# One Trainium2 core, a scan block and a window-attention block: first image's phase reordered, PSUM banks taken from the plan, three planned lengths changed

## The chip, the cores and the metric

The kernel runs on one core of one Trainium2 chip. The metric is the device time of one execution in microseconds. Engines are named as in the profile: PE (matmul; PEld is its weight load), DVE (vector), ACT (scalar), POOL (GpSimd) and SP, which issues most DMAs.

## The reference

Eight images of 192 channels, 64 x 64, float32, go through two layers.

Layer 0 widens 192 to 384 channels with a 1x1 product, convolves each channel 3x3, and derives from the result a 16-channel proxy. Four gates per direction and channel come from the proxy by 1x1 products. A recurrent scan then runs in four directions over chunks of eight columns:

```
x = conv1x1(x, W_in)
x = depthwise_conv3x3(x, W_dw) + b_dw
x_proxy = conv1x1(x, W_xd)
Gl, Gm, Gr = normalize_w(...)                  # each divided by |Gl|+|Gm|+|Gr|+eps
hn = l * x + gl * h_up + gm * h + gr * h_dn    # eight steps, four directions
out = out * Us + xs * Ds
y = einsum('bdchw,d->bchw', out_y, w_m); layernorm over channels; grn; conv1x1 to 192
```

Layer 1 is a layer norm, attention in 8 x 8 windows with six heads of 32 (the 16 largest scores of each row are kept, the others set to -100), a projection, a second layer norm, and a feed-forward part of 768 with gelu.

## The kernel before

**The first image's phase.** Image 0 is projected and convolved in a phase of its own, written out by hand. There are three blocks of 128 channels (`ct`) and four units of 16 rows (`u`), so twelve units. `projected` (L430 to L443) is four products into a PSUM tile `pin` (two buffers) and an ACT copy into the padded image `full`. `convolved` (L462 to L471) makes nine DVE steps of 1024 elements per partition into `acc` (three buffers). `convolved_by_products` (L473 to L484) makes the convolution with 18 products instead, each with a diagonal weight `dg`, into two PSUM tiles `pc`, emptied by ACT. `stored` (L446 to L457) copies `acc` twice with ACT, in two orders, and SP writes them to DRAM as `xsT` and `xs`. Nine units go to DVE, and the last three (`ct` 2, `u` 1 to 3) to PE. The loop at the end alternates: one projection, then the convolutions that have their rows; the three product units come last. The nine `dg` steps (L487) stand ahead of the loop on ACT's queue. Weights are loaded by `load`, which takes SP's and ACT's queue in turn.

**The weight work (L504 to L576).** In pools of its own, behind the phase: `w_cv` from `w_dw`, factors put into `w_g2` and `w_out`, and bias rows made by small products on PE (`bias_row`) and written back into the weight tiles by SP.

**The planned part.** Everything after that is written as steps with an engine, a planned length, what they read and what they write. `Plan.order` simulates the engines with these lengths, 60 times with adapted ranks, keeps the shortest plan and emits the steps sorted by planned start. Each engine then runs its instructions in that order. `front(b)` projects and convolves image b by way of DRAM (L650, L653, L696), `scan(b)` makes eight steps of twelve tiles (gates and outputs by L809, gate arithmetic L858 to L942, sums L968 to L990, `norm` L1003 to L1068), and `windows(b)` handles 8 rows of windows. The scan of image b stands beside the windows of image b-1 and the front of image b+1, so the first scan has no windows beside it and the last windows have no scan.

**PSUM.** Six banks (`l_ps`) serve all tiles of `bank()` under the tag "lp", two more (`n_ps`) the gate tile `nb`. The plan gives each new tile the bank that comes free first in its own times, but the program only asks the pool for the next buffer of that tag. The planned lengths are in nanoseconds:

```
vec = lambda n: (n / 0.96 + 69, 88)
act = lambda n, more=50.0: (n / 1.2 + more, 110)
gp = lambda n: (n * 2.3 + 52, 42)
```

`gp(512)` is the planned length of L897, L914, L918, L929, L980, L982, L988, L1406, L1423 and L1438; `mask` (L1393, L1396) is planned with 1500.

Of the kernel before, what the change touches and what calls it, by code (L numbers as in the profile page):

```python
# [31 lines left out]
P = 128  # L32
# [22 lines left out]
class Held:  # L55


    def __init__(self, pool, shape, name, bufs=None, tag=None, dtype=F32):
        self.args = pool, shape, dtype, name, tag or name, bufs or pool.bufs
        self.tag, self.bufs = (id(pool), tag or name), bufs or pool.bufs  # L60
        self.users, self.left, self.end, self.next, self.tile = [], 0, 0.0, None, None

    def make(self):
        if self.tile is not None:
            return
        pool, shape, dtype, name, tag, bufs = self.args
        self.tile = pool.tile(shape, dtype, name=name, tag=tag, bufs=bufs)

    def __call__(self):
# [10 lines left out]
class Plan:  # L80
# [67 lines left out]
    def order(self):  # L148

        before = [s.before for s in self.steps]
        tiles = {h: h.left for s in self.steps for h in s.held}
        best = None
        for n in range(self.RUNS):
            for s, k in zip(self.steps, before):
                s.before, s.ready = k, 0.0  # L160
            for h, k in tiles.items():
                h.left, h.end, h.next = k, 0.0, None
            run = self.run()
            if best is None or self.length < best[0]:
                best = self.length, run, [s.start for s in run]
            for s in run:
                needs = [d.start for d in s.after] + [h.next.start for h in s.held if h.next]
                rank = min(needs, default=s.end) - (s.end - s.start)
                s.rank = (s.rank + rank) / 2 if n else rank
        self.length, run, starts = best  # L170
        for s, t in zip(run, starts):
            s.start = t
        return run

    def run(self):
# [20 lines left out]
        for s in self.steps:  # L196
            for h in s.makes:
                queues.setdefault((h.tag, s.lane), []).append(s)
                slots.setdefault(h.tag, [(0.0, k, None) for k in range(h.bufs)])
        first = {k: 0 for k in queues}  # L200

        def kept(tag):
# [58 lines left out]
        while todo:  # L261
            for e in dirty_plain:
                best_plain[e] = picked(e, None, plain[e], ready)
            for e in dirty | dirty_plain:
                best[e] = picked(e, best_plain[e], makers[e], room)
            dirty_plain, dirty = set(), set()
            e = min((x for x in engines if best[x]), key=lambda x: best[x][1])
            _, t, s = best[e]
            s.start = t
            if e == "PE":  # L270
                lead, cycles, share = s.cost
                end = stream(t + lead, cycles, share)
                free[e], s.end = end, end + 140.0
            else:
                hold, more = s.cost
                free[e] = t + hold
                s.end = free[e] + more
            (makers if s.makes else plain)[e].remove(s)
            dirty_plain.add(e)
            todo -= 1  # L280
            done.append(s)
            for tag in needs.get(s, ()):
                first[tag, s.lane] += needs[s][tag]
            for h in s.makes:
                slot = min(slots[h.tag], key=lambda x: x[:2])
                slots[h.tag].remove(slot)
                if slot[2]:
                    slot[2].next = s
            touched = bool(s.makes)
            for h in s.held:  # L290
                h.left -= 1
                h.end = max(h.end, s.end)
                if not h.left:
                    slots[h.tag].append((h.end + self.HOP, h.users[0].n + h.bufs, h))
                    touched = True
            for d in s.after:
                d.before -= 1
                d.ready = max(d.ready, s.end + (self.HOP if d.engine != e else 30.0))
                if not d.before:
                    wake(d)  # L300
                    if not d.makes:
                        dirty_plain.add(d.engine)
                    elif d.lane:
                        dirty.add(d.engine)
                    else:
                        touched = True
            if touched:
                dirty.update(engines)
# [10 lines left out]
def tile_ss2d_then_window_attention(ctx: ExitStack, tc: tile.TileContext, a: dict, out: bass.AP):  # L319
# [8 lines left out]

    const = ctx.enter_context(tc.tile_pool(name="const", bufs=1))

    queues = [nc.sync, nc.scalar]
    n_loads = 0

    def load(name, src=None, rows=None):

        nonlocal n_loads
        src = a[name] if src is None else src
        shape = list(src.shape)
        t = const.tile([rows or shape[0]] + shape[1:], F32, tag=name, name=name)
        if rows:  # L340
            nc.gpsimd.memset(t[HALF:rows], 0.0)
        queues[n_loads % 2].dma_start(t[0 : shape[0]], src)
        n_loads += 1
        return t

    def blank(name, shape, value=None, engine=nc.gpsimd):
# [12 lines left out]
    ident = blank("ident", [P, P])  # L359
    make_identity(nc, ident)  # L360

    w_in = load("w_in")
    w_dv = load("w_dv")
    xa = epool.tile([P, H, W], F32, name="xa")
    xb = epool.tile([P, NG // 2, 8, W], F32, name="xb")
    for u in range(NG // 2):
        nc.sync.dma_start(xa[:, 16 * u : 16 * u + 16, :], x[0, 0:P, 16 * u : 16 * u + 16, :])
        for k in range(2):
            row = 16 * u + 8 * k
            nc.scalar.dma_start(xb[64 * k : 64 * k + 64, u], x[0, P:DM, row : row + 8, :])  # L370
        if u == 0:
            vecs = load("vecs")
    full = [epool.tile([P, H + 2, W + 2], F32, name=f"full{ct}") for ct in range(CT)]
    for t in full:
        nc.vector.memset(t[:, 0 : H + 2 : H + 1, :], 0.0)
# [50 lines left out]
        h.make()  # L426
    with early, tc.tile_pool(name="early_ps", bufs=2, space=PSUM) as early_ps:

        taps = [(dy, dx) for dy in range(3) for dx in range(3)]
        dg = epool.tile([P, 9, P], F32, name="dg")  # L430

# [30 lines left out]
        def convolved(ct, u):  # L462

            acc = epool.tile([P, 16, W], F32, name="acc", bufs=3)
            for n, tap in enumerate(taps):
# [2 lines left out]
                    nc.vector.tensor_scalar(acc, near(ct, u, *tap), w, b_dw[:, ct : ct + 1], ALU.mult, ALU.add)  # L468
                else:
                    nc.vector.scalar_tensor_tensor(acc, near(ct, u, *tap), w, acc, ALU.mult, ALU.add)  # L470
            stored(ct, u, acc)  # L471

        def convolved_by_products(ct, u):  # L473

            acc = epool.tile([P, 16, W], F32, name="acc", bufs=3)
            for k in range(2):
                pc = early_ps.tile([P, CH, W], F32, name="pc")
                for n, (dy, dx) in enumerate(taps):
# [4 lines left out]
                nc.scalar.activation(acc[:, 8 * k : 8 * k + 8, :], pc, AF.Identity, bias=b_dw[:, ct : ct + 1])  # L483
            stored(ct, u, acc)  # L484

        for n in range(9):
            nc.scalar.activation(dg[:, n, :], ident, AF.Copy, scale=w_dv[:, CT - 1, n : n + 1])  # L487
        units = [(ct, u) for ct in range(CT) for u in range(NG // 2)]
        by_vector = [(ct, u) for ct, u in units if ct < CT - 1 or u == 0]
        by_tensor = [c for c in units if c not in by_vector]  # L490
        done = 0
        for ct, u in units:
            projected(ct, u)
            while done < len(by_vector) and by_vector[done] < (ct, u):
                convolved(*by_vector[done])
                done += 1
            while by_tensor and by_tensor[0] < (ct, u):
                convolved_by_products(*by_tensor.pop(0))
        for c in by_tensor:
            convolved_by_products(*c)  # L500
        assert done == len(by_vector)

    with tc.tile_pool(name="prep", bufs=2) as prep, tc.tile_pool(name="prep_ps", bufs=2, space=PSUM) as prep_ps:

        w_dw = prep.tile([3 * RG, CT * 4 * 3], F32, name="w_dw")
        nc.sync.dma_start(w_dw, a["w_dw"])
        id3 = prep.tile([3 * RG, RG], F32, name="id3")
        nc.vector.tensor_add(id3, ident[0 : 3 * RG, 0:RG], ident[0 : 3 * RG, RG : 2 * RG])
        nc.vector.tensor_add(id3, id3, ident[0 : 3 * RG, 2 * RG : 3 * RG])
# [17 lines left out]
        def bias_row(name, dst, products, *more):  # L527

            n = dst.shape[-1]
            row = prep.tile([1, n], F32, name="row_" + name)  # L530
            nc.sync.dma_start(row, a[name])
            for at in range(0, n, 384):
                m = min(384, n - at)
                ps = prep_ps.tile([P, 512], F32, name="ps_pre")
# [3 lines left out]
                    )  # L538
                nc.vector.tensor_add(row[:, at : at + m], row[:, at : at + m], ps[0:1, 0:m])
            for extra in more:  # L540
                got = prep.tile([1, n], F32, name="more_" + name)
                nc.sync.dma_start(got, a[extra])
                nc.vector.tensor_add(row, row, got)
            nc.sync.dma_start(dst[HALF : HALF + 1, 1, :], row)


        bias_row("b_qk", w_qk, [(n1_b[:, ci : ci + 1], w_qk[0:HALF, ci, :]) for ci in range(2)])
# [39 lines left out]
    plan = Plan()  # L587
    vec = lambda n: (n / 0.96 + 69, 88)
    act = lambda n, more=50.0: (n / 1.2 + more, 110)
    gp = lambda n: (n * 2.3 + 52, 42)  # L590
    mm = lambda slots, n, share=0.96: (65.0, slots * n * 4.16, share)
    tiled = lambda cycles, share=1.0: (150.0, cycles, share)
    split = (275.0, 6475.0, 0.95)
# [550 lines left out]
    def window_row(b, g, z, sc, bb):  # L1144
# [225 lines left out]
        for r in range(3):  # L1370
# [21 lines left out]
            def mask(rng=rng, less=less):  # L1392
# [4 lines left out]
                    at()[:, rng, :], less(), neg.unsqueeze(1).to_broadcast([P, WS, 64])  # L1397
                )

            plan("DVE", (1500.0, 80.0), mask, r=kths, w=[less, (at, r)])  # L1400

            part = lambda rng=rng: at()[:, rng, :]
            plan(
# [15 lines left out]
            each = lambda v: v.unsqueeze(2).to_broadcast([P, WS, 64])  # L1419
            plan(  # L1420
                "POOL",
                gp(512),
                lambda part=part, rng=rng, each=each: nc.gpsimd.tensor_add(part(), part(), each(down()[:, rng])),  # L1423
                r=[(down, r)],
                w=[(at, r)],
# [3 lines left out]
            def denominators(part=part, rng=rng):  # L1429
# [4 lines left out]

            plan(
                "POOL",
                gp(512),
                lambda part=part, rng=rng, each=each: nc.gpsimd.tensor_mul(part(), part(), each(rd()[:, rng])),  # L1438
                r=[(rd, r)],
                w=[(at, r)],  # L1440
# [332 lines left out]
```

## Time and profile before

| what | value |
|---|---|
| median of 3 runs | 7621.01 us (7610.15 to 7637.82) |
| the profiled execution | 7623.82 us; its span 7622.0 us |
| mean granted PE clock | 0.86 |
| busy, share of the span | PE 88%, DVE 83%, POOL 82%, ACT 64% |
| first scan product (L809) to the last | 221.99 to 7066.16 us |
| DRAM traffic | 433.98 MB read, 226.18 MB written |

A line of the profile gives the source line, the engine, the operation, the tile written and the tiles read (buffer numbers left out). In answers in order of time the first two columns are start and duration, and the brackets hold the idle time ahead and what ended it. SPq and ACTq are DMA issues of those queues. Durations of single instructions overlap the next by some tens of ns, so a chain is read from start to start.

### The profile page before, as it was taken

The numbers are of one execution on the slowest core, as the hardware profiler recorded it, in microseconds if no ns is written. First come the engines' busy times: TensorE is split into PE (matmuls) and PEld (weight loads), VectorE is DVE, ScalarE is ACT, GpSimd is POOL, SyncE is SP. The second block draws the span as 40 slices with busy tenths as digits, with TensorE's granted clock in tenths as the row PEclk, the third lists the DMA queues.
The fourth block names the chain that finished last, engine by engine and source line by source line (L and its number), as shares of the span: only waits on it lengthen the run. The fifth ranks groups of instructions, "written<-read, shape, count | busy, mean of one in ns | idle before, by whom it ended". The sixth has DMA issues, their size and how long they took to land. (4 is left out here: it accounts for less than half of the span.)

```text
span 7622.0 us, 141764 instructions
## 1 busy us (share of the span) xinstructions
PE 6699.8 (88%) x50180; PEld 3458.4 (45%) x50180; DVE 6364.3 (83%) x15477; ACT 4896.1 (64%) x9649; POOL 6229.7 (82%) x6333
## 2 busy tenths in 40 slices
PE   5888789988998899888999899988888888888987
PEld 2333344444444444444444444444444444444554
DVE  5687788998899988988888988889899989889643
ACT  2455456765776657675777757766576756666665
POOL 0688888998899988988888888889899989899422
PEclk7888789987988889898998889988888878888999
DMA  3666455312551245312551135411211111111100
GB/s 107 164 174 163 121 139 135 101 51 75 154 145 46 55 134 151 89 46 78 157 139 47 50 105 143 124 50 46 60 50 50 49 59 52 49 45 45 32 22 14
DMA packets 988331, 669.39 MB, mean 88 GB/s; under 512 B 651972, under 2 KB 814215, under 8 KB 987623
## 3 DMA queue, kind: packets, MB, share of 16 engines
q1 hardware_dynamic: 985638, 656.86, 32.1%
q8 instruction: 398, 6.52, 0.4%
q10 hardware_dynamic: 1984, 3.48, 0.2%
q14 instruction: 311, 2.54, 0.1%
HBM read 433.98 MB, written 226.18 MB: 87 GB/s over the span
## 5 line engine op out<-in xcount | busy, mean ns | idle before, releaser
L809 PE MATMUL g<-xe,w_g 32*128 32x512 f32 x3648 | 1171.5, 749 | 224.4 <-DVE dx L968 74.6
L809 PE MATMUL g<-xo,w_g 32*128 32x512 f32 x3648 | 1189.1, 729 | 184.5 <-DVE dx L968 90.9
L866 ACT ACTIVATE ab<-g 128x512 f32<-128x512 f32 x1344 | 784.6, 596 | 393.0 <-PE nb L809 168.9
L897 POOL TENSOR_TENSOR ab<-ab 128x512 f32<-128x512 f32 x672 | 865.0, 1287 | 162.7 <-ACT ab L866 151.0
L929 POOL TENSOR_TENSOR pw<-pw,rr 128x512 f32<-128x512 f32 x672 | 867.4, 1291 | 135.6 <-ACT rr L912 115.4
L914 POOL TENSOR_TENSOR pw<-pw,pq 128x512 f32<-128x512 f32 x672 | 881.0, 1311 | 82.5 <-DVE pq L873 53.2
L918 POOL TENSOR_TENSOR pw<-pw,pq 128x512 f32<-128x512 f32 x672 | 878.1, 1307 | 15.5
L982 POOL TENSOR_TENSOR dx<-dx,hu 128x512 f32<-128x512 f32 x576 | 742.9, 1298 | 112.1 <-DVE hu L973 97.1
L910 ACT ACTIVATE rr<-nb,eps 128x512 f32<-128x512 f32 x672 | 462.0, 687 | 571.7 <-DVE nb L907 569.1
L809 PEld LDWEIGHTS g<-xo,w_g 32*128 32x128 f32 x3648 | 410.5, 208 | 719.3 <-DVE dx L968 192.9
L809 PEld LDWEIGHTS g<-xe,w_g 32*128 32x128 f32 x3648 | 408.9, 212 | 704.8 <-DVE dx L968 173.1
L1628 PE MATMUL lp<-hd,w_f 128*64 128x256 f32 (+1 forms) x2304 | 594.9, 497 | 56.1 <-ACT hd L1614 15.0
L990 POOL TENSOR_TENSOR y<-y,dx 128x512 f32<-128x512 f32 x384 | 597.6, 1563 | 2.2
L696 PE MATMUL lp<-strip,w_cv 128*32 128x256 f32 x8064 | 563.5, 418 | 27.6 <-DMA strip<-pad 19.2
L925 DVE SCALAR_TENSOR_TENSOR nb<-nb,rr 128x512 f32<-128x512 f32 x672 | 464.8, 692 | 142.5 <-ACT rr L912 140.3
L934 DVE SCALAR_TENSOR_TENSOR nb<-nb,pw 128x512 f32<-128x512 f32 x672 | 464.7, 692 | 138.4 <-POOL pw L929 136.2
L907 DVE TENSOR_TENSOR nb<-nb,ab 128x512 f32<-128x512 f32 x672 | 465.3, 692 | 113.1 <-POOL ab L897 103.5
L973 DVE TENSOR_TENSOR hu<-g,hid 128x512 f32<-128x512 f32 x768 | 518.7, 681 | 1.0 <-PE g L809 0.7
L809 PE MATMUL nb<-xe,w_g 32*128 32x512 f32 x672 | 479.1, 800 | 12.5 <-DVE hid L942 12.3
L888 ACT ACTIVATE nb<-nb 128x512 f32<-128x512 f32 x672 | 399.5, 594 | 137.7 <-DVE pq L875 78.2
L980 POOL TENSOR_TENSOR y<-hu,dx 128x512 f32<-128x512 f32 x192 | 246.3, 1289 | 291.7 <-DVE hu L973 289.7
L809 PE MATMUL nb<-xo,w_g 32*128 32x512 f32 x672 | 463.1, 774 | 14.6 <-DVE hid L942 14.6
(221 smaller groups left out, 16684.8 us busy)
## 6 DMA issues: line engine op xcount, KB each, us to landing
strip<-pad SPq DMA_DIRECT2D x1008, 132.0 KB
xd<-xsT SPq DMA_DIRECT2D x384, 256.0 KB
x<-xs SPq DMA_DIRECT2D x64, 768.0 KB
xd<-xs SPq DMA_DIRECT2D x192, 256.0 KB
z<-y SPq DMA_DIRECT2D x64, 768.0 KB
zg<-z SPq DMA_DIRECT2D x64, 768.0 KB
pad<-xin SPq DMA_DIRECT2D x168, 264.0 KB
xsT<-sn SPq DMA_DIRECT2D x168, 256.0 KB
```

Of the source, the lines that this page charges most:

```text
L696: nc.tensor.matmul(pc()[q * RG : (q + 1) * RG, k * 256 : (k + 1) * 256].rearrange("p (h w) -> p h w", h=4), lhsT=w_cv[:, ct, q, dx, :], rh ...
L809: nc.tensor.matmul(dst, lhsT=w[rows, col : col + P], rhs=xp[rows, :], start=True, stop=True)
L866: lambda r=r: nc.scalar.activation(ab()[:, r, :], g[r](), AF.Abs),
L897: plan("POOL", gp(512), lambda: nc.gpsimd.tensor_add(ab()[:, 0, :], ab()[:, 0, :], ab()[:, 1, :]), w=[ab])
L907: plan("DVE", vec(512), lambda: nc.vector.tensor_add(nb(), nb(), ab()[:, 0, :]), r=[ab], w=[nb])
L914: plan("POOL", gp(512), lambda: nc.gpsimd.tensor_add(one(), one(), pq()[:, 0, :]), r=[(pq, 0)], w=[pw])
L918: lambda: nc.gpsimd.tensor_add(one(), one(), pq()[:, 1, :]),
L929: plan("POOL", gp(512), lambda: nc.gpsimd.tensor_mul(one(), one(), rr()), r=[rr], w=[pw])
L973: lambda: nc.vector.tensor_mul(like(hu(), d), like(pu(), d), state(d, ct)),
L982: plan("POOL", gp(512), lambda: nc.gpsimd.tensor_add(dx(), dx(), hu()), r=[hu], w=[dx])
L990: nc.gpsimd.tensor_add(y, y, dx().rearrange("p (c i) -> p i c", c=CH))
L1628: nc.tensor.matmul(dst[:, at : at + rhs.shape[-1]], lhsT=lhsT, rhs=rhs, **flags)
```

## The change

Three edits, made together. Some helper lines move by a few; from the planned steps on (L600) the line numbers are the same in both.

1. *The first image's phase.* `load` uses SP's queue for all but `w_in`, `w_dv` and `vecs`, which go with the `xb` loads on ACT's. All twelve projections come first, with the `dg` steps behind the fourth. Then come the nine DVE convolutions, each followed by its store, and the three product units are put behind the 5th, 7th and 8th of them, with an own tag for their `acc`. The weight work keeps no pools of its own: it uses the phase's PSUM pool, and `w_dw` and the bias vectors are loaded early. The bias rows go back to the weight tiles from ACT's queue.
2. *The banks.* The plan notes which of the six banks it gave each tile (`slot`), and the program takes a tag with one buffer for each bank ("lp0" to "lp5").
3. *The lengths.* `gp` has 2.34 ns per element; the two POOL steps with a broadcast vector (L1423, L1438) get `gp_each` with 1.86; the mask is planned with 1700.

```diff
         pool, shape, dtype, name, tag, bufs = self.args
+        if tag == "lp":
+            tag, bufs = f"{tag}{self.slot}", 1
         self.tile = pool.tile(shape, dtype, name=name, tag=tag, bufs=bufs)
...
-                best = self.length, run, [s.start for s in run]
+                best = self.length, run, [s.start for s in run], {h: h.slot for h in tiles}
...
                 slot = min(slots[h.tag], key=lambda x: x[:2])
                 slots[h.tag].remove(slot)
+                h.slot = slot[3]
...
-        queues[n_loads % 2].dma_start(t[0 : shape[0]], src)
-        n_loads += 1
+        queue.dma_start(t[0 : shape[0]], src)
...
-    w_in = load("w_in")
-    w_dv = load("w_dv")
+    w_in = load("w_in", queue=nc.scalar)
+    w_dv = load("w_dv", queue=nc.scalar)
...
-        for n in range(9):
-            nc.scalar.activation(dg[:, n, :], ident, AF.Copy, scale=w_dv[:, CT - 1, n : n + 1])
...
-        for ct, u in units:
+        for n, (ct, u) in enumerate(units):
             projected(ct, u)
-            while done < len(by_vector) and by_vector[done] < (ct, u):
-                convolved(*by_vector[done])
-                done += 1
-            while by_tensor and by_tensor[0] < (ct, u):
-                convolved_by_products(*by_tensor.pop(0))
-        for c in by_tensor:
-            convolved_by_products(*c)
...
+            if n == 3:
+                for m in range(9):
+                    nc.scalar.activation(dg[:, m, :], ident, AF.Copy, scale=w_dv[:, CT - 1, m : m + 1])
+        for n, c in enumerate(by_vector):
+            acc = convolved(*c)
+            stored(*c, acc)
+            if n in (4, 6, 7):
+                convolved_by_products(CT - 1, (4, 6, 7).index(n) + 1)
...
-            nc.sync.dma_start(dst[HALF : HALF + 1, 1, :], row)
+            nc.scalar.dma_start(dst[HALF : HALF + 1, 1, :], row)
...
-    gp = lambda n: (n * 2.3 + 52, 42)
+    gp = lambda n: (n * 2.34 + 52, 42)
+    gp_each = lambda n: (n * 1.86 + 52, 42)
...
-            plan("DVE", (1500.0, 80.0), mask, r=kths, w=[less, (at, r)])
+            plan("DVE", (1700.0, 80.0), mask, r=kths, w=[less, (at, r)])
...
                 "POOL",
-                gp(512),
+                gp_each(512),
                 lambda part=part, rng=rng, each=each: nc.gpsimd.tensor_add(part(), part(), each(down()[:, rng])),
```

## The prediction

> **What bounds the kernel now.** I read first the page's slices, then the busy time by stage, then the first 225 us of each engine in order of time, then the table of waits.
>
> Busy time by stage (columns: stretch, its length, then busy us and count of PE, weight loads, DVE, ACT and POOL, the granted clock, the DMA share, GB/s):
>
> ```profile
> 27.00:130.00 103.00, 52.67 (x85) 17.30 (x86) 99.10 (x81) 31.96 (x35) 0.00 (x0) 0.66 0.31 86
> 130.00:178.00 48.00, 45.92 (x112) 19.40 (x110) 0.00 (x0) 17.29 (x21) 0.00 (x0) 1.00 0.26 73
> 178.00:200.00 22.00, 9.80 (x34) 7.79 (x35) 9.52 (x29) 0.98 (x1) 0.00 (x0) 0.50 0.24 69
> 222.00:7066.00 6844.00, 6099.80 (x45550) 3108.80 (x45546) 5995.59 (x14084) 4481.60 (x8816) 6046.00 (x5941) 0.86 0.34 92
> 7066.00:7622.00 556.00, 470.40 (x4312) 297.43 (x4302) 258.74 (x1276) 356.25 (x762) 168.93 (x357) 0.93 0.10 22
> ```
>
> There are three regimes. In the long middle PE is busy 89%, POOL 88% and DVE 88%: no engine alone is the bound, and a stall in one shows in the others. The last 556 us are window rows that hang on PE. Before 222 us one engine at a time is at work: DVE's convolution, then PE's, then small weight work. POOL is empty there, and whatever this stretch loses the end loses too. In order of time (DVE, then ACT, PE and SP; start, duration, what, and the idle time ahead with its releaser):
>
> ```profile
> 27.42 0.81 DVE L468 TENSOR_SCALAR acc<-full,w_dv,vecs 128x1024 f32<-128x1024 f32 x1 [25.28 <-ACT full L443]
> 28.27 10.60 DVE L470 SCALAR_TENSOR_TENSOR acc<-full,w_dv,acc 128x1024 f32<-128x1024 f32 x8
> ...
> 181.33 0.19 DVE L508 TENSOR_TENSOR id<-ident 96x32 f32<-96x32 f32 x1 [51.74 <-DMA xs<-st]
> ...
> 200.09 0.36 DVE L576 TENSOR_TENSOR rpb<-rpb,top_b 128x192 f32<-128x192 f32 x1
> ```
>
> ```profile
> 22.46 1.28 ACT L487 ACT_TABLE_LOAD   x1 [22.46 <-DMA temp<-in_temp_dram]
> ...
> 27.44 3.78 PE L439 MATMUL pin<-xa,w_in 128*128 128x512 f32 x4 [12.84 <-ACT full L443]
> ...
> 32.23 1.98 PE L439 MATMUL pin<-xa,w_in 128*128 128x512 f32 x4
> ```
>
> ```profile
> 122.15 18.02 PE L480 MATMUL pc<-full,dg 128*128 128x512 f32 x36 [5.31 <-ACT full L443]
> ...
> 142.87 31.17 PE L480 MATMUL pc<-full,dg 128*128 128x512 f32 x72
> ```
>
> ```profile
> 200.47 0.59 SPq L762 DMA_DIRECT2D x<-xs  x1
> ```
>
> Read: DVE starts its nine convolutions at 27.42, because ACT could not copy a projection out before it had issued its share of the weight loads (until 22.46). It ends them at 129.6 and then stands idle 51.7 us, until PE's three units are done and stored. The weight work runs 181.33 to 200.45, and the scan's first load leaves 0.02 us later. The waits (us, times, longest):
>
> ```profile
> PEld g L809 <- DVE dx L968: 366.0, 289, 8.7
> ...
> PE g L809 <- DVE dx L968: 165.5, 110, 7.1
> ```
>
> A gate product has no data from dx: PE waits here for the PSUM bank that dx reads.
>
> **Edit 1, the first image.** (a) *Start of DVE.* ACT's queue keeps w_in, w_dv, vecs and the eight xb loads, which it had issued by 8.79 us. It loses nine issues, the wait to 22.46, and the nine dg activations (2.74 us, now behind the fourth copy). PE's first two units end at 11.6 and 14.6 us today. A copy is 1.05 us, so the second one ends near 15.7 and DVE starts at 15.8: 11.6 us gained. Bounds: 0, if the now longer run of loads on SP's queue holds xa back, and 14. I take 11.6, since xa stands ahead of the weights there.
> (b) *The nine convolutions.* Unchanged: 27.42 to 129.6 is 102.2, so they end at 118.0. ACT copies all twelve projections before it stores the first result. By the warm row a unit takes 1.98+1.13, so the last copy is near 46 and the first store ends at 49, just before DVE's fourth unit (49.9) needs that acc buffer. Full cover; at the cold 3.78+1.2 throughout it would cost up to 18 us.
> (c) *The idle 51.7 us.* Gone if PE's units fit below DVE. The two pc banks are emptied only behind the 5th, 7th and 8th store on ACT (in-order): the second unit runs about 76 to 94, the third about 99 to 117, taking the 18.02 of the row that starts after a pause. The bias products follow, 1.45 us; DVE wants them 7 us into its weight work, at 125. Cover about 6 us.
> (d) *The weight work.* 181.33 to 200.45 is 19.1; the waits for w_dw (1.36) and the n1_br row (0.52) go, as both are loaded early: 17.2. New end 118.0+17.2 = 135.2.
> (e) *Gate to the scan.* ACT's last stores end near 124; the last one landed 3.6 us after its issue at 177.70, so 128 is before 135. The two bias rows now leave from ACT's queue, behind which only the table load and the first xin copy stand; SP is free for xt, and PE's last weight product ends about 2 us before DVE. From the x load on the instruction order is as before.
> Sum: 200.5-135.2 = 65 us. I take -64, bounds -45 (a or c half lost) and -68.
>
> For (c) there is a rule that speaks against the change. The row: four products take 3.78 us after a pause and 1.98 in the next run, and 36 take 18.02 after a pause but 15.6 (half of 31.17) behind it. The Trainium skill (TensorE: Matmul & The Clock Gate, Part 1) says that the array runs at half rate until some 3.4 us of sustained work and falls back after an idle window of that length; pulling the three units apart then buys two more cold starts, an estimate of 1.7 us each by its figures, against 2.4 by the rows. By either the cost lies on PE, below DVE.
>
> **Edit 2, the banks.** No instruction changes. Before, the pool hands out banks by its own turn; now each tile gets the bank the plan gave it. Put to the traced execution (same order, same times), 932 of 6360 tiles get another predecessor. The time by which a bank's last reader ends after PE's previous instruction sums to 505 us with the pool's choice, 474 with the plan's, and 461 if always the earliest were taken. So most bank waits are true shortage, and 31 us can go. Bounds: 0 (PE would wait for DVE or POOL anyway, both 88% busy) and -31. A loss isn't excluded where the real release order differs from the plan's; the 13 us between plan and earliest bound that. I take -15, half.
>
> **Edit 3, the planned lengths.** Nothing runs longer or shorter; the planner writes another order. In the trace a POOL 512-step followed at once takes 1.23 us from start to start (median; mean 1.24 to 1.28), against 1.23 planned before and 1.25 now; the two steps with a broadcast vector 1.00 (1.23, now 1.00); the mask 1.53 (median; mean 1.72) against 1.50, now 1.70. Planned POOL time moves by 3840x0.0205 = +79 and 384x0.2253 = -87 us: it sums to nothing, so I book no gain. In the new order, behind the last gate product 312 of the last product's rows are left instead of 286: half a window row, +8 us of PE work by the rows' medians (402 against 394). The stretch after it took 556 us for 394, so +11; if PE bounds the middle that work is saved there, so 0 to +11. I take +5. The new order's luck in the middle I bound by POOL's busy time in fifteen 400 us stretches from 800 to 6800: mean 354, standard deviation 10.9. Fifteen independent ones give 10.9x3.9 = 42 us; part of that is common to both orders, so it is an upper bound.
>
> **Sum.** 7623.8 (the profiled execution, span 7622.0) -64-15+5 = 7549.8. The profiled one is 2.8 above the median of the three, so 7547.
>
> **Rivals.** *The new order interlocks worse (slower).* Place: 222 to 7066. Price: POOL's work is fixed at 6046; at 87% busy instead of 88.3% it takes 105 us longer, and 7547+105 = 7652. It decides from about 97 us, 1.4% of the stretch. For it: two stretches (800 and 1600) ran at 85%, and everything on five engines is reordered. Against: it needs over twice the upper bound above, and the image-by-image progress of PE's work in the new order is within 20 us of the old.
> *The head's gain is half taken by a new wait.* PE's third unit, emptied late and cold throughout (0.86 us a row instead of 0.43, so 31 us for its 36), would end near 141 and hold the bias rows: the scan starts near 154 instead of 135, 19 lost: 7566; with (a) lost as well, 7578.
> *The bank edit does nothing*, because a freed bank only lets PE reach the next wait sooner: 7562.
>
> **Numbers.** About 0.3% (23 us) is what a measurement here can tell from no change. Forecast 0.72 (7500 to 7590), head half lost 0.12 (7566 to 7600), worse interlock 0.16: of it 0.08 beyond +23 us, 0.06 within, 0.02 below. Two hundredths of the second case also reach the band: faster 0.84, same 0.08, slower 0.08. The range takes the spread of 42 around 7547, with the unknown ends of (a) and edit 2 above: 7496 to 7604.
>
> **What would show it.** Right: DVE's first convolution at 15 to 17 us, no idle stretch after the ninth, the first x load near 135, the first gate product near 157; waits of L809 on L968 down by some 30 of 531 us. Wrong: DVE starting above 22, a DVE wait for the bias product above 5 us; POOL's share in the middle below 87%; a tail above 580 us.

## The result, and the profile after

The changed kernel takes 7596.51 us (median of 7 runs, 7591.85 to 7605.62) against 7630.99 for the kernel before (7 runs). The ratio is 0.996, 95% interval 0.9947 to 0.9972: faster by 0.4%, where 1.0% was forecast. The profiled execution took 7596.51 us, span 7594.7.

Busy time by stage of the changed kernel (columns as in the prediction), cut at the same events:

```profile
16.00:118.00 102.00, 82.72 (x194) 31.83 (x193) 99.12 (x83) 46.43 (x57) 0.00 (x0) 0.90 0.50 139
118.00:135.00 17.00, 10.46 (x38) 8.07 (x38) 8.99 (x28) 6.12 (x7) 0.00 (x0) 0.58 0.89 263
...
152.40:7015.40 6863.00, 6102.77 (x45395) 3104.10 (x45392) 6012.23 (x14081) 4475.57 (x8805) 6043.42 (x5936) 0.85 0.34 92
7015.40:7594.70 579.30, 494.48 (x4459) 309.31 (x4456) 261.98 (x1280) 362.51 (x774) 170.59 (x361) 0.91 0.10 22
```

PE now works under DVE's convolution (82.72 us instead of 52.67), and the 48 us in which PE alone was at work are gone. The middle, from the first gate product to the last, takes 6863 us instead of 6844, and the stretch after it 579 instead of 556, with 4459 matmul rows in it instead of 4312. So the gain at the start is 222.0-152.4 = 69.6 us, and at the end of the trace 27.3 of it are left: 19 went in the middle, 23.5 in the last stretch.

The first 153 us of DVE, in order of time:

```profile
14.82 1.12 DVE L477 TENSOR_SCALAR acc<-full,w_dv,vecs 128x1024 f32<-128x1024 f32 x1 [12.68 <-DMA xb<-in_x_dram]
...
106.50 10.53 DVE L479 SCALAR_TENSOR_TENSOR acc<-full,w_dv,acc 128x1024 f32<-128x1024 f32 x8
116.94 0.18 DVE L510 TENSOR_TENSOR id<-ident 96x32 f32<-96x32 f32 x1
...
132.93 0.16 DVE L568 TENSOR_TENSOR b_f<-b_f,ps_pre 128x6 f32<-128x6 f32 x1 [5.44 <-PE ps_pre L565]
...
134.44 0.36 DVE L575 TENSOR_TENSOR rpb<-rpb,top_b 128x192 f32<-128x192 f32 x1
153.53 0.69 DVE L842 TENSOR_TENSOR hid<-g,x 128x512 f32<-128x512 f32 x1 [18.73 <-PE g L809]
```

DVE starts at 14.8 (before 27.4) and goes from the ninth convolution into the weight work with no idle time (before 51.7 us). The product units, the last weight products and the first products of the planned part, on PE:

```profile
45.05 15.72 PE L489 MATMUL pc<-full,dg 128*128 128x512 f32 x36
75.41 17.89 PE L489 MATMUL pc<-full,dg 128*128 128x512 f32 x36 [14.63 <-ACT acc_p L492]
97.95 18.56 PE L489 MATMUL pc<-full,dg 128*128 128x512 f32 x36 [4.65 <-ACT acc_p L492]
...
126.66 6.23 PE L565 MATMUL ps_pre<-n_gb,w_f 128*128 128x1 f32 x24
133.19 3.75 PE L650 MATMUL lp<-xt,w_in 128*128 128x512 f32 x4 [0.30 <-issue]
...
152.37 7.99 PE L809 MATMUL g<-xe,w_g 32*128 32x512 f32 x28
```

The second and third unit start after a pause and take 2.2 and 2.8 us more than the first: the first five and seven of their products start 0.67 to 1.02 us apart, the others 0.43. They end at 116.5, just inside DVE's cover. On SP's queue the scan's first load leaves at 127.8, before the weight work has ended:

```profile
127.80 0.59 SPq L762 DMA_DIRECT2D x<-xs  x1
```

The two waits shown before, in the changed kernel:

```profile
PEld g L809 <- DVE dx L968: 320.3, 281, 9.5
...
PE g L809 <- DVE dx L968: 127.5, 103, 8.6
```

They fell from 531 to 448 us, more than the 30 that the prediction named as a sign of the bank edit. But the fall came from the new order. With edits 1 and 2 (planned banks, old order) the same waits are these, one line number lower:

```profile
PEld g L808 <- DVE dx L967: 380.3, 295, 8.6
...
PE g L808 <- DVE dx L967: 175.5, 113, 7.1
```

With edits 1 and 3 (the pool's banks, new order), six line numbers lower:

```profile
PEld g L803 <- DVE dx L962: 324.4, 297, 8.5
...
PE g L803 <- DVE dx L962: 123.3, 96, 7.7
```

That is 556 and 448 us; with edit 1 alone they sum to 541, with edit 2 alone to 558. The bank edit did not shorten this wait, and the sign that was named for it came true by another edit.

### The profile page after: what moved, and what is told of

It reads as the page before. It is cut to its first block, busy times and chain, and to the rows that moved or that the text cites. A ratio compares the mean times of both kernels' runs of the same rounds, so it can differ in the third digit from the quotient of the medians.

```text
span 7594.7 us, 141716 instructions
## 1 busy us (share of the span) xinstructions
PE 6711.4 (88%) x50180; PEld 3461.2 (46%) x50180; DVE 6384.4 (84%) x15477; ACT 4896.9 (64%) x9649; POOL 6229.2 (82%) x6333
## 4 chain that ended last, share of the span: by engine, by line
PE 26%; DVE 26%; POOL 23%; ACT 11%; issue 5%; DMA 1%; SPq 0%; POOLq 0%; ACTq 0%; DVEq 0%
PE g L809 7%; PE lp L1628 5%; POOL ab L897 4%; POOL pw L929 4%; POOL pw L914 3%; POOL dx L982 3%; POOL pw L918 3%; DVE rest L1381 2%; POOL y L990 2%; DVE nb L934 2%; DVE dx L968 2%; PE lp L696 2%; DVE nb L907 2%; PE lp L1594 2%; DVE hu L973 1%
## 5 line engine op out<-in xcount | busy, mean ns | idle before, releaser
L809 PE MATMUL g<-xe,w_g 32*128 32x512 f32 x3648 | 1190.5, 749 | 207.1 <-DMA xe<-flat 43.4
L1628 PE MATMUL lp<-hd,w_f 128*64 128x256 f32 (+1 forms) x2304 | 613.9, 508 | 48.9 <-ACT hd L1614 22.1
L925 DVE SCALAR_TENSOR_TENSOR nb<-nb,rr 128x512 f32<-128x512 f32 x672 | 464.1, 691 | 178.3 <-ACT rr L912 175.9
L942 DVE TENSOR_TENSOR hid<-lx,nb 128x512 f32<-128x512 f32 x672 | 454.4, 676 | 4.7
```

The source lines that it names most:

```text
L809: nc.tensor.matmul(dst, lhsT=w[rows, col : col + P], rhs=xp[rows, :], start=True, stop=True)
L1628: nc.tensor.matmul(dst[:, at : at + rhs.shape[-1]], lhsT=lhsT, rhs=rhs, **flags)
```

## Experiments

All ratios are to the kernel before, measured with it, from 4 to 12 runs of each kernel and 7 to 23 of the kernel before.

**The three edits taken apart.** Theory A: the start gives its full gain, and the order that the new lengths wrote gives half of it back. Theory B: an earlier scan is given back whatever the order. Theory C: the planned banks cost what is missing.

*Edit 1 alone* (the whole of the first image's phase and the weight work as changed; `make`, `order` and all lengths as before):

```diff
+        for n, c in enumerate(by_vector):
+            acc = convolved(*c)
+            stored(*c, acc)
+            if n in (4, 6, 7):
+                convolved_by_products(CT - 1, (4, 6, 7).index(n) + 1)
```

> Edit 1 alone, with the order and the banks of before. Theory A (the first image's phase gives its full gain, and the order that the new lengths wrote gives half of it back): 65 to 72 us below before, ratio about 0.991, the first gate product near 152 and the stages behind it as long as before to within 5 us each. Theory B (an earlier first scan is given back later whatever the order): 30 to 40 us, ratio near 0.9955.

Measured: 7562.92 us, ratio 0.9905 (0.9892 to 0.9918). The first gate product is at 153.0, the middle takes 6851 us and the last stretch 555.9 (before 6844 and 555.8). So the first gate product comes 69 us earlier, and the traced span is 62 us shorter; the middle is 7 us longer, 2 more than theory A allowed. By the ratio the start is worth about 72 us (62 to 82). Theory B, which asked for 30 to 40, falls.

*Edit 2 alone:*

```diff
+        if tag == "lp":
+            tag, bufs = f"{tag}{self.slot}", 1
```

> Edit 2 alone, with the order of before. Theory A: 0 to 20 us below before, ratio 0.9975 to 1.000, and the time by which banks come free behind PE's previous instruction sums to some 475 us instead of 505. Theory C (the planned banks themselves cost what is missing): slower by 25 us or more, ratio above 1.003.

Measured: 7617.7 us, ratio 0.9978 (0.9968 to 0.9988), some 17 us faster. Theory C falls. What makes the 17 us is less sure. The twelve runs go from 7604 us to 7639 us, and their times go with the granted clock, 0.859 to 0.866 (correlation -0.85), which in the kernel before was 0.857 to 0.863. The one execution that was traced, at 0.859, has a span of 7625.1 us, 3 us longer than before.

*Edits 1 and 2* (against the whole change):

```diff
-    gp = lambda n: (n * 2.34 + 52, 42)
-    gp_each = lambda n: (n * 1.86 + 52, 42)
+    gp = lambda n: (n * 2.3 + 52, 42)
...
-            plan("DVE", (1700.0, 80.0), mask, r=kths, w=[less, (at, r)])
+            plan("DVE", (1500.0, 80.0), mask, r=kths, w=[less, (at, r)])
```

> Edits 1 and 2, with the planned lengths and so the order of before. Theory A: 70 to 90 us below before, ratio 0.988 to 0.991, and so about 40 us faster than the changed kernel. Theory B and theory C: no better than the changed kernel, ratio 0.995 or above.

Measured: 7555.38 us, ratio 0.9892 (0.9879 to 0.9905). Its two long stages (middle, then last stretch):

```profile
153.10:6996.30 6843.20, 6100.59 (x45554) 3110.14 (x45554) 5996.52 (x14085) 4474.06 (x8816) 6038.59 (x5942) 0.86 0.34 92
6996.30:7553.10 556.80, 472.22 (x4302) 298.30 (x4302) 258.59 (x1276) 356.05 (x762) 168.38 (x356) 0.92 0.10 22
```

Both are as long as in the kernel before. Against the whole change the middle is 20 us shorter and the last stretch 22.5, with 157 matmul rows fewer in it.

*Edits 1 and 3* (against the whole change; the pool's own banks):

```diff
-        if tag == "lp":
-            tag, bufs = f"{tag}{self.slot}", 1
```

> Edits 1 and 3, with the pool's own choice of banks. Theory A: 15 to 35 us below before (the head's 69 less some 40 that the new order costs), ratio 0.9955 to 0.998. Theory C: 60 us or more below before, ratio under 0.992.

Measured: 7614.67 us, ratio 0.9976 (0.9966 to 0.9985). So edit 3 costs 0.9976-0.9905 = 0.0071 with the pool's banks and 0.996-0.9892 = 0.0068 with the plan's, about 53 us either way (49 and 42 us by the traced spans); the banks gain 0.0013 to 0.0022 (10 to 17 us) in three pairs, of which the two pairs with edit 1 have intervals that overlap. Theory A holds.

**Which of the lengths, or any length?** Theory E: one of the new lengths is wrong for the plan. Theory D: any touch of a length makes the planner write another order, orders differ by some tens of us, and this change drew a bad one. These kernels have edits 1 and 2.

*A length changed below what anyone could measure:*

```diff
-    gp = lambda n: (n * 2.3 + 52, 42)
+    gp = lambda n: (n * 2.301 + 52, 42)
```

> Edits 1 and 2, and the planned POOL length raised by 0.001 ns per element (512 elements: 0.5 ns), which no measurement of a step could tell. Theory D (the order of before is one of the better of many that the planner may write, and any touch of a length draws another): 15 to 60 us slower than edits 1 and 2 with the old lengths (ratio to before 0.991 to 0.997). Theory E (the new lengths are themselves the worse ones): within 10 us of them, ratio 0.988 to 0.9905.

Measured: 7591.19 us, ratio 0.9942 (0.9929 to 0.9956). Half a nanosecond in 1230 costs 0.005, 38 us. Theory D's number.

*The POOL length alone*, for all its lines:

```diff
-    gp = lambda n: (n * 2.3 + 52, 42)
+    gp = lambda n: (n * 2.34 + 52, 42)
```

> Edits 1 and 2, and of the lengths only the POOL step at 2.34 ns per element, for all of its lines. Theory E with the POOL length as the cause: ratio near 0.996, as the changed kernel. Theory D: anywhere in 0.989 to 0.998, with no relation to the other single lengths.

Measured: 7540.51 us, ratio 0.9877 (0.9864 to 0.9891).

*The mask alone:*

```diff
-            plan("DVE", (1500.0, 80.0), mask, r=kths, w=[less, (at, r)])
+            plan("DVE", (1700.0, 80.0), mask, r=kths, w=[less, (at, r)])
```

> Edits 1 and 2, and of the lengths only the mask at 1700. Theory E with the mask as the cause: ratio near 0.996. Theory D: anywhere in 0.989 to 0.998.

Measured: 7552.27 us, ratio 0.99 (0.9886 to 0.9915).

*The mask at 1700 and the broadcast steps at 1.86* (against the whole change):

```diff
-    gp = lambda n: (n * 2.34 + 52, 42)
+    gp = lambda n: (n * 2.3 + 52, 42)
```

> Edits 1 and 2, the mask at 1700 and the two broadcast POOL steps at 1.86, the common POOL length at its old 2.3. Theory E with these two as the cause: ratio near 0.996, and the one with the POOL length alone near 0.989. Theory D: anywhere in 0.989 to 0.998.

Measured: 7522.27 us, ratio 0.9854 (0.9838 to 0.9871), the fastest of all kernels here, ahead of both the kernel before and the changed one. Its stages:

```profile
152.90:6969.40 6816.50, 6099.88 (x45778) 3089.78 (x45776) 6011.81 (x14162) 4492.98 (x8864) 6048.41 (x5961) 0.86 0.35 93
6969.40:7511.60 542.20, 453.70 (x4078) 283.50 (x4074) 245.77 (x1199) 340.76 (x715) 164.34 (x336) 0.92 0.10 22
```

More window work stands beside the scans (45778 matmul rows instead of the changed kernel's 45395), and yet the middle is 46 us shorter; the last stretch has 381 rows fewer and is 37 us shorter. Neither the POOL length nor the mask alone, nor the mask with the broadcast steps, comes near 0.996, and the effects do not add: -0.0015 for the POOL length and -0.0038 for the other two, but +0.0068 for all three. Theory E falls for what was run; the broadcast steps alone were not. Theory D, too, was off in one point: it took the old order for one of the better ones and expected 0.989 to 0.998, and 0.9877 and 0.9854 lie below that.

**The three lengths together.** Theory F: only the three together make a bad plan, whatever the last digit. First the whole change with one length touched each time. *The common POOL length:*

```diff
-    gp = lambda n: (n * 2.34 + 52, 42)
+    gp = lambda n: (n * 2.341 + 52, 42)
```

> The whole change, with the POOL length at 2.341 instead of 2.34. Theory D (each touch of a length draws another order, and the change drew a bad one): another time than the changed kernel's 0.996, more likely better than not, 0.985 to 0.996. Theory F (the three new lengths together make a worse plan, whatever the last digit): 0.9945 to 0.9975.

Measured: 7534.98 us, ratio 0.9862 (0.9842 to 0.9882).

*The mask:*

```diff
-            plan("DVE", (1700.0, 80.0), mask, r=kths, w=[less, (at, r)])
+            plan("DVE", (1701.0, 80.0), mask, r=kths, w=[less, (at, r)])
```

> The whole change, with the mask at 1701 instead of 1700. Theory D: 0.985 to 0.996, more likely better than the changed kernel. Theory F: 0.9945 to 0.9975.

Measured: 7564.76 us, ratio 0.9905 (0.989 to 0.9919).

*The broadcast steps:*

```diff
-    gp_each = lambda n: (n * 1.86 + 52, 42)
+    gp_each = lambda n: (n * 1.861 + 52, 42)
```

> The whole change, with the two broadcast POOL steps at 1.861 instead of 1.86. Theory D: 0.985 to 0.996, more likely better than the changed kernel. Theory F: 0.9945 to 0.9975.

Measured: 7569.57 us, ratio 0.9913 (0.9898 to 0.9928). All three neighbours of the change are outside theory F's band and inside theory D's, and better than the change itself.

*Edits 1 and 2 with the old lengths, the POOL one touched:*

```diff
-    gp = lambda n: (n * 2.3 + 52, 42)
+    gp = lambda n: (n * 2.299 + 52, 42)
```

> Edits 1 and 2 with the old lengths, the POOL length at 2.299 instead of 2.3. Theory D: 0.985 to 0.996, the mean of all such draws near 0.990. Theory F: near the 0.9892 of the untouched old lengths, within 0.0015.

Measured: 7550.27 us, ratio 0.989 (0.9873 to 0.9906). By its time this run doesn't tell the theories apart. But it isn't the same order: its stages are 6813 and 578 us where the untouched lengths gave 6843 and 557.

```profile
153.20:6966.50 6813.30, 6071.89 (x45406) 3087.41 (x45406) 6016.11 (x14083) 4476.96 (x8807) 6044.19 (x5932) 0.86 0.34 93
6966.50:7544.90 578.40, 486.56 (x4450) 307.48 (x4450) 260.18 (x1278) 362.42 (x772) 173.59 (x365) 0.90 0.10 22
```

**The ten orders side by side**, all with edits 1 and 2 (middle: first to last gate product of the profiled execution; last: from there to the end; rows: matmul records that start in it):

| lengths | ratio | middle us | last us | rows in last |
|---|---|---|---|---|
| each and mask new | 0.9854 | 6816 | 542 | 4074 |
| changed, gp 2.341 | 0.9862 | 6825 | 559 | 4290 |
| gp 2.34 only | 0.9877 | 6832 | 550 | 4170 |
| old, gp 2.299 | 0.9890 | 6813 | 578 | 4446 |
| old | 0.9892 | 6843 | 557 | 4298 |
| mask 1700 only | 0.9900 | 6811 | 588 | 4475 |
| changed, mask 1701 | 0.9905 | 6854 | 555 | 4168 |
| changed, each 1.861 | 0.9913 | 6856 | 557 | 4430 |
| old, gp 2.301 | 0.9942 | 6858 | 578 | 4438 |
| **changed** | **0.9960** | 6863 | 579 | 4456 |

Their mean is 0.98995 and their standard deviation 0.0033, 25 us. The changed kernel has the longest middle of the ten and the second longest last stretch. Its interval (0.9947 to 0.9972) overlaps that of gp 2.301 (0.9929 to 0.9956); all others are clear of it. The last stretch goes with the rows left in it (correlation 0.88, about 0.09 us a row); the middle's length doesn't go with the last one's (correlation -0.01), so a good order has to be lucky twice. What in an order makes its middle long was not settled: in the four middles shown above the busy times of PE, DVE and POOL are each equal to within 0.6%. Among DVE's waits the largest difference is at L925, for ACT's L912: in the middle 144 us with the old lengths, 176 in the changed kernel and 126 in the fastest. Over the ten it goes with the middle's length (correlation 0.74), but gp 2.34 only has 166 us of it beside a middle of 6832, so it is no more than a hint. The change has the highest ratio of these ten, 2.5 standard deviations above the other nine (mean 0.9893, standard deviation 0.0027). That this was chance rather than a cause of its own is argued from its three neighbours, not shown further.

## Why the prediction was right or wrong

**Edit 1** was forecast at -64 and gave -69.6 in the trace, -72 by the ratio of the kernel with it alone. (a) DVE started at 14.8, forecast 15.8. (b) The nine convolutions took 102 us; ACT's first store ended at 49.05 and DVE began its fourth unit at 49.21, so the cover was as thin as said, and held. (c) The third product unit ended at 116.5, forecast 117, and DVE did not wait for a bias product at its first use. Its longest wait for one, 5.44 us at L568, is above the 5 us named as a sign of being wrong, but it was there before, with 4.95 us. Of the rule weighed there (the Trainium skill, TensorE: Matmul & The Clock Gate, Part 1) the direction holds: each unit after a pause paid a cold start, 2.2 and 2.8 us in the trace, nearer to the 2.4 of the rows than to the 1.7 by the page's figures. It cost nothing, as DVE covered it. (d) The weight work ran from 116.94 to 134.80, 17.9 us for the 17.2 worked out. (e) was wrong in its gate, on the good side: the x load did not wait for DVE's last weight step, but left 7 us ahead of it, and PE's last weight product at 132.9 with the xt products behind it became the gate. The first gate product came at 152.4 instead of 157.

**Edit 2** was forecast at -15 between 0 and -31. The three pairs gave -10, -12 and -17, so the size was near; that it came by way of the bank waits is shown only in part. Count in every trace, for each tile, by how much the last reader of the tile before it in its bank ends behind the PE record ahead of its own first product. By this count the prediction's 505, 474 and 461 are 526, 492 and 476. The three pairs:

| pair | waiting us | above the earliest bank |
|---|---|---|
| before, and edit 2 alone | 526, 516 | 50, 19 |
| edit 1, and edits 1 and 2 | 538, 512 | 56, 20 |
| edits 1 and 3, and the whole change | 515, 495 | 53, 20 |

The avoidable part fell by 31 to 36 us, as worked out, but what no choice of bank avoids rose by 10 to 21, so that 10 to 26 us went. And the pair with the largest gain in time, 17 us, has the smallest fall, 10 us; there the clock differed as well.

**Edit 3 is the term that was mis-sized.** "I take +5" for the last stretch, and nothing for the middle; it cost 53 by the ratios, 42 to 49 in the traces. It failed in two places. First, the half window row left behind the last gate product was priced by the medians of its lines: +8 us of PE work, +11 at most. It took 22.5. The trace has 157 matmul rows more there. At the mean of 470.4/4312 = 0.109 us they are 17 us of PE, and at PE's 85% share there 20; at the 0.09 us a row of the ten orders they are 14. So the medians priced the row too low, but the rows alone may not make 22.5: the granted clock was lower there too, 0.91 for 0.92, and what that added was not separated. Second, the new order's luck in the middle was taken as zero with a bound of 42 us; it was 20 us against edits 1 and 2. The runs give that luck its size: a standard deviation of 20 us for the middle and 25 us for the whole time. So the bound was good and the range held the time; the point forecast, 7547 us, a ratio of 0.9903, is the mean of ten draws to within 0.0004, and not what this one draw gave. That it meets the mean so closely is in part luck, as the start gave 6 to 8 us more than its term. The forecast's own case (7500 to 7590) had left too little room above.

**The rivals.** "The new order interlocks worse" named the right place, in its mild form: the middle became 19 us longer, and POOL's share of it fell from 88.3% to 88.1%, not to 87%, so the kernel stayed faster. With edits 1 and 2 and the old order the share is 88.2%, so it hardly tells the orders apart. The new wait on the third product unit did not appear. That the bank edit does nothing is unlikely, as all three pairs have one sign, but two of them have intervals that overlap and in the third the clock differed as well.

## What to carry to other kernels

When a planner orders the work, a change of any planned length is a new draw, whatever the length is worth: here 0.5 ns in 1230 moved the time by 38 us, more than the bank edit was worth. Keep such an edit apart from edits with a mechanism of their own, give it the spread of a few draws as its price, and pick the order by measuring several; here that was worth 74 us between the change as made and the best of ten. A sign that is named for one of several edits is to be read in a run of that edit alone: here the wait that should have told of the banks fell by the new order. The gain in a stretch where one engine works alone (the start here) arrived nearly whole: 69 us at the first gate product, 62 us in the traced span.

## What the runs showed of the hardware

The granted clock of one kernel differs between its executions, and its time with it: over the twelve runs of edit 2 alone the clock was 0.859 to 0.866 and the time 7604 to 7639 us. Kernels with one and the same order had mean clocks of 0.8594 (the kernel before, in 23 runs), 0.8622 (edit 2), 0.8635 (edit 1) and 0.8623 (edits 1 and 2).

The same 50180 matmul records kept PE busy for 6667 us in the traced execution of the fastest order and 6745 in that of the mask alone, with mean granted clocks of 0.8662 and 0.8594; other runs of the latter reached 0.864. Over the ten orders the mean clock of a kernel's runs goes with its ratio (correlation -0.72), and the kernels with the three new lengths ran lower (0.8582 and 0.8593) than the same edits with the old lengths (0.8635 and 0.8623). Whether an order lowers the clock, or the clock moved by itself and part of the cost that is put down to the order is the clock's, was not separated. In the last stretch of the changed kernel the granted clock was 0.91, with edits 1 and 2 alone 0.92.
